# A four-layer graph network on one core: norms on ScalarE, GpSimd for more of the scalings, and a new order of the work

## The chip, the cores and the metric

The kernel runs on one core of a Trainium2 chip. The core has a matrix engine (TensorE, PE in the profile, with its weight loads as PEld), VectorE (DVE), ScalarE (ACT), GpSimd (POOL) and the DMA queues, here those of SyncE (SP) and ScalarE. They run side by side and wait for each other by semaphores. The metric is the device time of one execution in microseconds (us): 2461.91 is the median of three runs of the kernel before, which lie between 2461.11 and 2462.0.

## The reference

There are 16 graphs (batches) of 1024 nodes with 128 features each, and a dense 1024x1024 array adj for each graph. Four layers follow one another; each adds its result to x:

```
h = relu(layernorm(x));  x = x + L0(h, adj)   # three times: h=hW+b; ew = adj * cos(h_i, h_k); h = ew @ h (relu but for the last)
h = relu(layernorm(x));  x = x + L1(h, adj)   # adj^T h + (1+eps) h, then two dense products with relu, masked by node
h = relu(layernorm(x));  x = x + L2(h, adj)   # softmax over neighbours of tanh(s1_i + s2_k); a node without any keeps h
h = relu(layernorm(x));  x = L3(h, adj) + x   # e = (hA)h^T + its transpose, softmax, times adj, relu -> h'
                                              # i,f,o = sigmoid([h, h'] w);  o * tanh(sigmoid(i*h' + f*h))
```

All is in float32. The four norms, the lone nodes of layer 2 and the last line of layer 3 are what the change touches.

## The kernel before

**Tiling.** The 1024 nodes are NB = 8 blocks of P = 128, one node per partition. A tile 128x1024 holds one array of 1024 nodes by 128 features, block beside block. adj of a graph is loaded twice: transposed by 32x32 squares with DMA and VectorE (adjT, `turn`, used by layers 0, 2 and 3), and as it is (adjL, layer 1).

**Stages.** `layer0` to `layer3` write down the operations of one batch, in a loop over 16 batches. Each of the three products of layer 0, and layer 3, walks over eight tiles j: TensorE makes a row of the square (sq, L753), VectorE multiplies it with adjT (ew, L952, or e, L1169), TensorE sums up (acc, L815 or L826). As the square is symmetric, half of its blocks are taken from those above: copied by ScalarE (above, L785) and turned by TensorE (L763), or, in batches 1 to 13, one quarter by VectorE and DMA (L775, by_hbm, got).

**Order.** Nothing is issued as it is written. `op`, with its short forms `pe`, `act`, `dve` and `pool_op`, hands each operation to `Plan` with an assumed duration. `Plan.order` (L137) then plays the engines through: at each step it takes, among the operations ready on the engine that is free first, the one of lowest rank (due time of its batch, less the work behind it, less a lead from the table `LEADS`), assigns slots of the buffers (`POOLS`, and in `KINDS` limits for each kind, in all and for younger batches) and so fixes each engine's instruction stream. Batches up to `AHEAD` = 2 after the oldest are open at once. The due times are `PERIOD` apart, the last one only `LAST` after the one before. A `dve` operation with a true last argument, and every `pool_op`, take one shared "port" in this plan, so that two of them are never planned at once.

**Norms.** `layernorm` (L653) takes statistics on VectorE (L663, L672), the power -0.5 on GpSimd (`power`, L555), nb = -mean * rstd on VectorE (L682), and then scales: blocks 0 to 3 by VectorE (`scale_by_vector`, L689, one TENSOR_SCALAR a block, L691), blocks 4 to 7 by ScalarE (`scale_by_scalar`, L696, one ACTIVATE a block with relu, L698). `relu` (L712) clips the first half on ScalarE where hn itself is used again (L719). A branch on the letter "R" in `FLAGS` (L702) does all eight on ScalarE.

**Lone nodes.** In `layer2`, x += hn * alone for nodes without neighbours: eight SCALAR_TENSOR_TENSOR of VectorE (`add_scaled`, L637), or, with "P", two instructions of GpSimd (`on_pool`, L647).

**The end of a batch.** In `layer3`, `finish` (L1225) computes the gates (L1237, L1261, L1262), z = hn * f on GpSimd (L1265), z += h' * i (`scaled`, L1244), two tanh on ScalarE (L1241, L1242), and z * o + x (`scaled` again). `scaled` is eight SCALAR_TENSOR_TENSOR (L1255) or, with "P" or in the last two batches (`late`, "y"), a multiply and an add of GpSimd (L1248, L1249). For the last batch `finish` runs twice, for half of the nodes each ("h"). In the last two batches GpSimd also does the product e * adjT of the odd j of layer 3 ("z", L1190), which is VectorE's otherwise (L1194).

The letters that hold before are:

```
    FLAGS = set("Cabcdkxhyz")
    PERIOD, LAST, AHEAD, WINDOW = 60.0, 9.0, 2, 0.05
```

Of the kernel before, what the change touches and what calls it, by code (L numbers as in the profile page):

```python
# [8 lines left out]
F32 = mybir.dt.float32  # L9
# [5 lines left out]
P = 128  # L15
# [207 lines left out]
def tile_adj_preln(  # L223
# [66 lines left out]

    R = B * NB
# [22 lines left out]
    eye3 = const.tile([D, E3], F32, name="eye3")  # L314
    load_const(third, b3e[:, 0:D], L3_W_b.partition_broadcast(P))
    for g, (w, v) in enumerate(((L3_ig_w, L3_ig_b), (L3_fg_w, L3_fg_b), (L3_og_w, L3_og_b))):
        at = slice(D + g, D + g + 1)
        load_const(third, w3e[:, at], w[0, 0:D].rearrange("(p o) -> p o", o=1))
        load_const(third, eye3[:, at], w[0, D : 2 * D].rearrange("(p o) -> p o", o=1))
        load_const(third, b3e[:, at], v.partition_broadcast(P))  # L320
    for load_it in first:
        load_it()
# [10 lines left out]
    POOLS = {"adjT": 16, "adjL": 5, "x": 3, "big": 13, "above": 2, "got": 1, "bank": 8, "small": 29, "row": 8, "hbm": 3, "hrow": 2}  # L333
    KINDS = {
        "adjT": ("adjT", 16, 16), "adjL": ("adjL", 5, 5), "x": ("x", 3, 3), "w4": ("big", 10, 6),
        "chunk": ("big", 12, 4), "above": ("above", 2, 1), "got": ("got", 1, 1), "ps": ("bank", 8, 8),
        "acc": ("bank", 8, 8), "small": ("small", 7, 6), "row": ("row", 4, 2), "hbm": ("hbm", 3, 2),
        "hrow": ("hrow", 2, 1),
    }
    PERIOD, LAST, AHEAD, WINDOW = 60.0, 9.0, 2, 0.05  # L340

    LEADS = {
        "0 ACT hT": 10, "0 ACT hn": -27, "0 DVE hn": -7.5, "0 DVE mv": 18.5, "0 DVE nb": -2, "0 DVE st": -7,
        "0 PE ps": 6, "0 POOL rstd": -23, "00 ACT above": -218, "00 ACT hT": 68.5, "00 ACT hTn": -53.5,
        "00 ACT sq": -48, "00 DMA by": 63.5, "00 DMA got": -27.5, "00 DVE above": -233, "00 DVE ew": -9,
        "00 DVE h": -18.5, "00 DVE ss": -111, "00 PE acc0": -166.5, "00 PE ps": -134, "00 PE psP": -26,
        "01 ACT above": 3.5, "01 ACT hT": 55, "01 ACT hTn": -8.5, "01 ACT sq": 54.5, "01 DMA by": -23,
        "01 DMA got": 26, "01 DVE above": 4, "01 DVE ew": 108.5, "01 DVE h": -56, "01 DVE ss": 126.5,
        "01 PE acc0": -136, "01 PE ps": 9, "01 PE psP": -303.5, "02 ACT above": 5, "02 ACT hTn": -115.5,
        "02 ACT sq": 6.5, "02 DMA by": 38, "02 DMA got": -41, "02 DVE above": -10.5, "02 DVE ew": -116,  # L350
        "02 DVE h": -5, "02 DVE ss": -17, "02 DVE x": -78, "02 PE acc0": -116, "02 PE ps": -15, "02 PE psP": 12,
        "02 PE sq": 175, "02 POOL rn": 47.5, "1 ACT g": -36, "1 ACT hn": -48.5, "1 ACT y1": -1.5,
        "1 DMA adjL": -41.5, "1 DVE adjL": -57, "1 DVE hn": -11.5, "1 DVE mv": -94, "1 DVE nb": 152,
        "1 DVE st": -539.5, "1 DVE x": 119.5, "1 PE acc1": -1, "1 PE py": -157, "1 PE py2": -10.5,
        "1 POOL rstd": -12, "2 ACT e2": -4, "2 ACT h": 114.5, "2 ACT hfl": -3.5, "2 ACT hn": -82,
        "2 ACT hnT": -9, "2 DVE alone": 5, "2 DVE e2": 105, "2 DVE h": -2.5, "2 DVE hn": 2.5,
        "2 DVE hrow": -74.5, "2 DVE mv": 11.5, "2 DVE nb": 36.5, "2 DVE rden": 26.5, "2 DVE st": -3,
        "2 DVE x": -11, "2 PE acc2": 5.5, "2 PE p1": 1.5, "2 PE pf": 22, "2 PE ps": 23.5, "2 PE psP": -299.5,
        "2 POOL rstd": 4.5, "3 ACT above": 93, "3 ACT e3": 29, "3 ACT gT": 13.5, "3 ACT gate": -70,
        "3 ACT h3T": -6, "3 ACT hn": 9, "3 ACT hnT": 66.5, "3 ACT hp": -371, "3 ACT hs": -94, "3 ACT z": -137,  # L360
        "3 DMA by": -47.5, "3 DMA got": 34.5, "3 DMA z": -167.5, "3 DVE above": 23.5, "3 DVE e3": -253.5,
        "3 DVE gate": -473.5, "3 DVE h": -119, "3 DVE hn": -0.5, "3 DVE mv": -27.5, "3 DVE nb": 25,
        "3 DVE st": -150, "3 DVE top": -14, "3 DVE z": -942, "3 PE acc3": -134, "3 PE pg": -81, "3 PE ps": 54,
        "3 PE psN": -465.5, "3 PE psP": 3.5, "3 PE sq": 73, "3 POOL rstd": -109.5, "3 POOL z": -13.5,
        "T ACT adjT": -44, "T DMA adjT": 10.5, "T DVE adjT": -411.5, "0 ACT hT <0": -20.5, "0 ACT hT <1": 6,
        "0 ACT hT >0": 6, "0 ACT hT >1": 12, "0 ACT hn <0": -3, "0 ACT hn <1": 49, "0 ACT hn >0": 0,
        "0 ACT hn >1": 31, "0 DVE hn <0": -146.5, "0 DVE hn <1": -18, "0 DVE hn >0": -50, "0 DVE hn >1": 34,
        "0 DVE mv <0": -8.5, "0 DVE mv <1": 29.5, "0 DVE mv >0": 4, "0 DVE mv >1": -11, "0 DVE nb <0": 27,
        "0 DVE nb <1": -61, "0 DVE nb >0": -16.5, "0 DVE nb >1": 51.5, "0 DVE st <1": -11.5, "0 PE ps <0": 25.5,
        "0 PE ps <1": 4, "0 PE ps >0": 9, "0 PE ps >1": 22, "0 POOL rstd <0": 35, "0 POOL rstd <1": 12.5,  # L370
        "0 POOL rstd >0": -77, "0 POOL rstd >1": -19.5, "00 ACT above <0": -4, "00 ACT above <1": -60,
        "00 ACT above >0": -198.5, "00 ACT above >1": -41.5, "00 ACT hT <0": 1.5, "00 ACT hT <1": 11,
        "00 ACT hT >0": 21.5, "00 ACT hT >1": -18, "00 ACT hTn <0": -28.5, "00 ACT hTn <1": 60.5,
        "00 ACT hTn >0": -127, "00 ACT hTn >1": -97.5, "00 ACT params <0": -7.5, "00 ACT sq <0": 223,
        "00 ACT sq <1": 321.5, "00 ACT sq >0": -46, "00 ACT sq >1": 179.5, "00 DMA by <1": 0.5,
        "00 DMA got <1": -76, "00 DMA params <0": 12, "00 DVE above <1": -159, "00 DVE ew <0": 0,
        "00 DVE ew <1": -57.5, "00 DVE ew >0": -155, "00 DVE ew >1": -235.5, "00 DVE h <0": -3,
        "00 DVE h <1": -148.5, "00 DVE h >0": 45, "00 DVE h >1": -2.5, "00 DVE params <0": 60,
        "00 DVE ss <0": 109, "00 DVE ss <1": 12.5, "00 DVE ss >0": -8.5, "00 DVE ss >1": -228.5,
        "00 PE acc0 <0": -64, "00 PE acc0 <1": -216.5, "00 PE acc0 >0": -246, "00 PE acc0 >1": -266.5,  # L380
        "00 PE params <0": 101, "00 PE ps <0": 0, "00 PE ps <1": -36.5, "00 PE ps >0": 39, "00 PE ps >1": -91.5,
        "00 PE psP <0": 20, "00 PE psP <1": -2, "00 PE psP >0": 47, "00 PE psP >1": -187.5, "00 PE sq <1": 51,
        "00 PE sq >0": -4, "00 PE sq >1": 3, "01 ACT above <0": 49.5, "01 ACT above <1": -68.5,
# [127 lines left out]

    FLAGS = set("Cabcdkxhyz")

    LO, HI = 1, 2
    TINY = 0.09  # L520
    STT = 0.262

    def V(n, scalar=False):
# [605 lines left out]
    def layer3(b, xt, aT):  # L1129
# [77 lines left out]
        for s, (lo, hi) in enumerate(HALVES):  # L1207
            evict(acc[s], hpT, lo, hi, AF.Relu)
# [185 lines left out]
```

## Time and profile before

| | us |
|---|---|
| time, median of three | 2461.91 |
| span of the profiled run | 2462.7 |
| TensorE busy | 2397.5 |
| VectorE busy | 2106.1 |
| ScalarE busy | 1291.5 |
| GpSimd busy | 254.5 |
| scaling of norms, VectorE / ScalarE (256 instructions each) | 73.1 / 105.3 |
| lone nodes on VectorE (128) | 34.9 |
| last scalings on VectorE (112 + 112) | 30.5 + 30.6 |
| z = hn * f on GpSimd (15 whole, 2 halves) | 28.6 + 2.0 |

How to read it: busy time is what an engine spends on instructions, and a high share of it marks the engine to look at first. Here TensorE works for 97% of the span, so time taken from another engine counts only where TensorE (or, at the end, the output) waits for it. The granted clock of TensorE is 0.991 of full speed over the span. DMA is never short but in the first 100 us, when the parameters and the first graphs arrive.

### The profile page before, as it was taken

The page shows a single profiled execution, that of the slowest core. Times are in us where ns is not written, and L with a number is a line of the kernel's source. Part 1 is how long each engine was busy: PE and PEld are TensorE (multiplying, and loading weights), DVE is VectorE, ACT ScalarE, POOL GpSimd, SP SyncE. Part 2 cuts the span into 40 slices and gives each one's busy share as a digit, 9 for nine tenths or more (in the row PEclk, how much of TensorE's full clock was granted, in tenths as well). Part 3 has the DMA queues.
Part 4 walks back from the last instruction along what each step waited for, and adds up shares of the span by engine and source line. Part 5 has one row for each costly group of instructions (what it writes and reads, how often), then busy time and mean ns, then how long its engine had stood idle before and what let it go on. Part 6 is the DMA issues. An engine that isn't in the chain of part 4 may idle for free.

```text
span 2462.7 us, 34845 instructions
## 1 busy us (share of the span) xinstructions
PE 2397.5 (97%) x11946; PEld 1592.9 (65%) x11946; DVE 2106.1 (86%) x5232; ACT 1291.5 (52%) x2404; POOL 254.5 (10%) x155
## 2 busy tenths in 40 slices
PE   6999999999999999999999999999999999999985
PEld 3568576775756657576675766657576675765763
DVE  6758889888998989899898998989899898897585
ACT  4415564735546465464644646465464745656274
POOL 1001010100101101010010101101010010100025
PEclk9999999999999999999999999999999999999998
DMA  8731929658394764928649394774929646072000
GB/s 132 125 103 35 167 56 144 139 89 160 72 159 112 107 142 94 174 67 147 136 82 167 65 164 114 100 145 93 173 73 146 134 86 133 28 96 75 26 1 18
DMA packets 1129473, 263.35 MB, mean 107 GB/s; under 512 B 971856, under 2 KB 1112912, under 8 KB 1129296
## 3 DMA queue, kind: packets, MB, share of 16 engines
q1 hardware_dynamic: 1108368, 251.73, 57.3%
q10 hardware_dynamic: 20928, 9.40, 1.4%
q8 instruction: 94, 1.54, 0.3%
q14 instruction: 83, 0.68, 0.1%
HBM read 198.14 MB, written 62.91 MB: 106 GB/s over the span
## 4 chain that ended last, share of the span: by engine, by line
PE 86%; DVE 5%; DMA 4%; ACT 3%; SPq 1%; POOL 1%; issue 0%; POOLq 0%; DVEq 0%; ACTq 0%
PE acc L815 33%; PE sq L753 17%; PE acc L826 17%; PE psP L593 6%; PE sq L763 4%; PE py L1014 2%; PE py L603 2%; PE ps_hTn L562 2%; DMA adjT<-in_adj_dram 1%; DMA by_hbm<-above 1%; PE ps_hnT L562 1%; PE pg L603 1%; DVE ew L952 1%; PE psN L593 1%; SPq L872 1%; DMA got<-by_hbm 1%
## 5 line engine op out<-in xcount | busy, mean ns | idle before, releaser
L952 DVE SCALAR_TENSOR_TENSOR ew<-sq,rn,adjT 128x512 f32<-128x512 f32 x612 | 437.9, 741 | 92.8 <-ACT above L785 33.0
L815 PE MATMUL acc<-ew,h 128*128 128x512 f32 x1024 | 488.0, 598 | 8.6 <-DVE ew L952 8.3
L753 PE MATMUL sq<-hTn 128*128 128x512 f32 (+3 forms) x1152 | 432.3, 488 | 0.4 <-ACT hTn L615 0.3
L785 ACT COPY above<-sq 128x384 f32<-128x384 f32 (+3 forms) x432 | 167.6, 392 | 431.8 <-PE sq L763 257.4
L753 PEld LDWEIGHTS sq<-hTn 128*128 128x128 f32 x1152 | 198.8, 191 | 152.6 <-issue 104.3
L815 PEld LDWEIGHTS acc<-ew,h 128*128 128x128 f32 x1024 | 177.7, 191 | 164.8 <-issue 120.9
L555 POOL TENSOR_TENSOR rstd<-ve,mhalf 128x8 f32<-128x8 f32 x64 | 107.5, 1679 | 1572.5 <-DVE ve L674 1524.3
L826 PEld LDWEIGHTS acc<-h,ew 128*128 128x128 f32 x2048 | 243.1, 192 | 29.9 <-issue 17.3
L826 PEld LDWEIGHTS acc<-h,e 128*128 128x128 f32 x2048 | 240.5, 194 | 25.6 <-issue 13.3
L826 PE MATMUL acc<-h,ew 128*128 128x128 f32 x2048 | 252.3, 276 | 0.9 <-DVE ew L952 0.9
L826 PE MATMUL acc<-h,e 128*128 128x129 f32 x2048 | 243.1, 277 | 3.4 <-DVE e L1102 3.4
L815 PE MATMUL acc<-e,hs 128*128 128x512 f32 x512 | 242.1, 595 | 0.5 <-DVE e L1194 0.5
L883 ACT ACTIVATE adjT<-adjT 128x1024 f32<-128x1024 f32 x128 | 135.2, 1057 | 203.8 <-DVE adjT L880 136.2
L815 PE MATMUL acc<-adjL,hn 128*128 128x512 f32 x512 | 229.6, 593 | 0.1
L763 PEld LDWEIGHTS sq<-ident,above 128*128 128x128 f32 x960 | 125.2, 141 | 122.1 <-issue 79.2
L1185 ACT ACTIVATE e<-e,top 128x1024 f32<-128x1024 f32 x128 | 146.8, 1147 | 105.3 <-DVE top L1181 103.6
L763 PE MATMUL sq<-ident,above 128*128 128x128 f32 x960 | 175.5, 274 | 5.5 <-ACT above L785 5.4
L1102 DVE SCALAR_TENSOR_TENSOR e<-adjT,e 128x512 f32<-128x512 f32 x256 | 161.5, 685 | 14.6 <-ACT e L1098 14.4
L880 DVE STREAM_TRANSPOSE adjT<-adjT 128x1024 f32<-128x1024 f32 x128 | 154.5, 1223 | 14.5 <-DMA adjT<-in_adj_dram 13.9
L775 DVE STREAM_TRANSPOSE above<-sq 128x512 f32<-128x512 f32 x208 | 147.3, 709 | 21.6 <-PE sq L753 19.6
L815 PEld LDWEIGHTS acc<-adjL,hn 128*128 128x128 f32 x512 | 93.9, 190 | 102.8 <-issue 88.1
L1194 DVE TENSOR_TENSOR e<-e,adjT 128x512 f32<-128x512 f32 x240 | 157.2, 686 | 0.0
(129 smaller groups left out, 3534.2 us busy)
## 6 DMA issues: line engine op xcount, KB each, us to landing
adjT<-in_adj_dram SPq DMA_DIRECT2D x512, 128.0 KB, 4.2
adjL<-in_adj_dram SPq DMA_DIRECT2D x128, 512.0 KB, 5.0
by_hbm<-above SPq DMA_DIRECT2D x104, 512.0 KB, 4.1
got<-by_hbm SPq DMA_DIRECT2D x416, 128.0 KB, 3.9
x<-in_x_dram SPq DMA_DIRECT2D x15, 512.0 KB, 5.4
out_dram<-z ACTq DMA_DIRECT2D x15, 512.0 KB, 5.9
x<-in_x_dram SPq DMA_DIRECT2D x2, 256.0 KB, 4.4
out_dram<-z ACTq DMA_DIRECT2D x2, 256.0 KB, 2.3
```

The costliest lines, as they stand in the source:

```text
L593: nc.tensor.matmul(dst.t[:, (c - lo) * n : (c - lo + 1) * n], cols(srcT.t, c), w, start=True, stop=True)
L753: lambda: nc.tensor.matmul(dst.t[:, (first - lo) * P :], cols(leftT.t, j), span(rightT.t, first, hi), start=True, stop=True),
L763: nc.tensor.transpose(cols(dst.t, r), cols(above.t, p), ident)
L775: lambda: nc.vector.transpose(span(above.t, p, p + 4), read.t),
L785: lambda: nc.scalar.copy(span(above.t, p, p + hi - first), read.t[:, (first - lo) * P :]),
L815: lambda s=s, lo=lo, hi=hi: nc.tensor.matmul(acc[s].t, cols(h.t, at, w), span(ew.t, lo, hi), start=(j == 0), stop=(j == NB - 1)),
L826: nc.tensor.matmul(a.t[:, (c - lo) * n : (c - lo + 1) * n], cols(ew.t, c), h.t[:, j * w : j * w + n], start=(j == 0 and c == lo), stop=(j ...
L880: dve(V(N), [t], [t], lambda t=t: nc.vector.transpose(t.t, t.t), True)
L952: lambda view=view, ew=ew, rn=rn, j=j, lo=lo, hi=hi: nc.vector.scalar_tensor_tensor(by_block(span(ew.t, lo, hi), D, 4), view(), rn.t[:, j ...
L1102: lambda e=e, j=j, lo=lo, hi=hi: nc.vector.scalar_tensor_tensor(span(e.t, lo, hi), span(aT[j].t, lo, hi), 0.0, span(e.t, lo, hi), op0=ALU. ...
L1185: lambda e=e, top=top, tot=tot: nc.scalar.activation(e.t[:, 0:N], e.t[:, 0:N], AF.Exp, bias=top.t, accum_out=tot.t),
L1194: lambda e=e, j=j, lo=lo, hi=hi: nc.vector.tensor_mul(span(e.t, lo, hi), span(e.t, lo, hi), span(aT[j].t, lo, hi)),
```

## The change

The letters in `FLAGS` become "CabcdkxhPRzT". "y" goes, and three come:

- R: all eight blocks of each norm are scaled by ScalarE, with the relu in the same instruction, so that `relu` has nothing left to do.
- P: GpSimd adds the lone nodes in layer 2 and does both scalings at the end of layer 3.
- T: the last batch is an exception to that. VectorE ends it, the product hn * f included, which becomes one TENSOR_SCALAR a block; and the odd tiles of e * adjT in its layer 3 return to VectorE (batch 14 leaves them on GpSimd).

This is meant to relieve VectorE in the middle of the kernel, and to spare the end GpSimd's long instructions. GpSimd's adds are now planned with 2.37 us in place of 1.9, and its products e * adjT with 2.45 in place of 1.96. The order is made anew: other slot limits, other due times, and new values for all of `LEADS`. Other branches that come with the diff ("E" with `by_nodes` and `share`, "u" and "v" in `far`) are off; with these letters `far` is true for the same batches 1 to 13 as the condition it replaces.

```diff
-    POOLS = {"adjT": 16, "adjL": 5, "x": 3, "big": 13, "above": 2, "got": 1, "bank": 8, "small": 29, "row": 8, "hbm": 3, "hrow": 2}
+    POOLS = {"adjT": 16, "adjL": 5, "x": 3, "big": 13, "above": 2, "got": 1, "bank": 8, "small": 24, "row": 5, "hbm": 3, "hrow": 2}
     KINDS = {
-        "adjT": ("adjT", 16, 16), "adjL": ("adjL", 5, 5), "x": ("x", 3, 3), "w4": ("big", 10, 6),
-        "chunk": ("big", 12, 4), "above": ("above", 2, 1), "got": ("got", 1, 1), "ps": ("bank", 8, 8),
-        "acc": ("bank", 8, 8), "small": ("small", 7, 6), "row": ("row", 4, 2), "hbm": ("hbm", 3, 2),
+        "adjT": ("adjT", 16, 16), "adjL": ("adjL", 5, 5), "x": ("x", 3, 3), "w4": ("big", 11, 7),
+        "chunk": ("big", 10, 8), "above": ("above", 2, 1), "got": ("got", 1, 1), "ps": ("bank", 7, 5),
+        "acc": ("bank", 8, 5), "small": ("small", 7, 7), "row": ("row", 5, 5), "hbm": ("hbm", 3, 2),
...
-    PERIOD, LAST, AHEAD, WINDOW = 60.0, 9.0, 2, 0.05
+    PERIOD, LAST, AHEAD, WINDOW = 90.0, 11.0, 2, 0.02
     LEADS = {
...
-    FLAGS = set("Cabcdkxhyz")
+    FLAGS = set("CabcdkxhPRzT")
...
-        pool_op(1.9, [a, b], [dst], lambda: nc.gpsimd.tensor_add(by_block(dst.t), v(), by_block(b.t)))
+        pool_op(2.37, [a, b], [dst], lambda: nc.gpsimd.tensor_add(by_block(dst.t), v(), by_block(b.t)))
...
-            if ("5" in FLAGS or "z" in FLAGS and b >= B - 2) and j % 2:
-                pool_op(1.96, [e, aT[j]], [e], lambda e=e, j=j: nc.gpsimd.tensor_mul(e.t[:, 0:N], e.t[:, 0:N], aT[j].t))
+            if ("5" in FLAGS or "z" in FLAGS and (b == B - 2 if "T" in FLAGS else b >= B - 2)) and j % 2:
+                pool_op(2.45, [e, aT[j]], [e], lambda e=e, j=j: nc.gpsimd.tensor_mul(e.t[:, 0:N], e.t[:, 0:N], aT[j].t))
...
-        late = b >= B - 2
+        late = b == B - 2 if "T" in FLAGS else b >= B - 2
+        final = "T" in FLAGS and b == B - 1
...
-                if "P" in FLAGS or ("y" in FLAGS and late):
+                if not final and ("P" in FLAGS or ("y" in FLAGS and late)):
...
-                    pool_op(us, [blk(a, lo, hi, w), blk(c, lo, hi)], [blk(z, lo, hi)], lambda: nc.gpsimd.tensor_add(part(z), part(a, w), part(c)))
+                    pool_op(us + 0.4 * n / NB, [blk(a, lo, hi, w), blk(c, lo, hi)], [blk(z, lo, hi)], lambda: nc.gpsimd.tensor_add(part(z), part(a, w), part(c)))
...
+            if final:
+
+                def of_x():
+                    for k in range(lo, hi):
+                        nc.vector.tensor_scalar_mul(cols(z.t, k), cols(hn.t, k), gate.t[:, 3 * k + 1 : 3 * k + 2])
+
+                dve(n * 0.17, [blk(hn, lo, hi), at], [blk(z, lo, hi)], of_x)
+            else:
+                pool_op(
+                    0.2 + 1.7 * n / NB, [blk(hn, lo, hi), at], [blk(z, lo, hi)],
+                    lambda: nc.gpsimd.tensor_mul(part(z), part(hn), per_node(of(1), n)),
+                )
```

## The prediction

> **What bounds the kernel now.** I read the page's busy table first, then the same table cut into stretches, then the chain of waits at the end, then the timeline around GpSimd's instructions.
>
> From the page, the row of engine totals:
>
> ```profile
> PE 2397.5 (97%) x11946; PEld 1592.9 (65%) x11946; DVE 2106.1 (86%) x5232; ACT 1291.5 (52%) x2404; POOL 254.5 (10%) x155
> ```
>
> Busy time of each engine by stretch (stretch, length, then PE, weight loads, DVE, ACT, POOL, with instruction counts; last the granted clock, DMA share, GB/s):
>
> ```profile
> 0.00:100.00 100.00, 78.51 (x322) 46.29 (x323) 73.12 (x171) 46.68 (x92) 12.16 (x13) 0.97 1.02 156
> ...
> 300.00:2100.00 1800.00, 1794.45 (x8933) 1189.43 (x8932) 1616.37 (x4021) 964.03 (x1800) 163.94 (x97) 1.00 0.66 120
> ...
> 2350.00:2400.00 50.00, 40.86 (x246) 32.72 (x245) 42.56 (x101) 37.03 (x62) 9.68 (x5) 0.90 0.00 1
> ...
> 2437.00:2463.00 26.00, 0.03 (x1) 0.00 (x0) 3.46 (x4) 5.67 (x10) 20.94 (x15) 0.55 0.14 40
> ```
>
> TensorE is full through the middle. It is short of work in three places: the first 100 us (21.5 idle), 2350 to 2400 (9.1 idle) and the last 26 us, when GpSimd works alone. The ends of matmuls are modelled, so I also added the start-to-start distances of all matmuls. In the chain 24 of the 512-wide ones take 10.30 us, 0.429 each, and 128 of the 128-wide take 14.29 us, 0.112 each. At its usual spacing (0.429, 0.322, 0.216 and 0.109 to 0.112 us by width) all TensorE work sums to 2359 us. The other 104 us are: 11.9 before the first matmul; 18 more lost in the first 100 us; 5 in 200 to 300; about 18 between 300 and 2100, or 1 us in each 148 us batch; 2 in 2100 to 2330; 15.6 around 2355 to 2395; 26 after the last matmul; and some 7 of jitter of a few ns.
>
> The end of the chain of waits (start, us, what), where GpSimd's 15 us begin:
>
> ```profile
> 2434.80 1.80 PE psN L593 x16
> ...
> 2436.62 0.50 ACT hp L1216
> ...
> 2437.14 1.72 DVE gate L1237
> ...
> 2439.12 1.61 DVE gate L1262
> ...
> 2440.78 2.16 POOL z L1249
> ...
> 2454.13 1.86 POOL z L1248
> ...
> 2456.04 2.37 POOLq L1390
> ```
>
> Fifteen GpSimd instructions run one behind another here: five for batch 14 (128x1024), ten for the two halves of batch 15. The two gate instructions on 128x12 take 1.7 and 1.6 us; that is no work but a wait for GpSimd.
>
> **What the Trainium skill says.** "GPSIMD Engine Reference", Specifications, says that GpSimd's SBUF interfaces are shared with VectorE, with contention for VectorE instructions in a 2-port mode or with two SBUF inputs. The trace agrees in part. Timeline (start, us, instruction):
>
> ```profile
> 2386.25 3.15 DVE L691 TENSOR_SCALAR hn<-x,mv,rstd 128x128 f32<-128x128 f32 x4
> ...
> 2386.41 2.38 POOL L1190 TENSOR_TENSOR e<-e,adjT 128x1024 f32<-128x1024 f32 x1 [0.70 <-PE sq L763]
> ```
>
> Four TENSOR_SCALAR take 3.15 us instead of some 1.1: one sits 2.38 us behind the GpSimd product. A TENSOR_TENSOR on adjL (L997, median 0.286) took 1.303 in the same position. But the 44 SCALAR_TENSOR_TENSOR of 128x128 that overlap GpSimd average 0.345 us, against a median of 0.344 for the others, although they too have two SBUF inputs. So I charge stalls to TENSOR_SCALAR and TENSOR_TENSOR only.
>
> The same page, Engine selection, puts elementwise work with two inputs at about twice VectorE's time. Here: multiply 1.91 and add 2.16 to 2.34 us, 4.2 us a pair, for what eight VectorE instructions at 0.26 spacing do in 2.1. It agrees.
>
> "ScalarE: Activation LUTs", What ACT_TABLE_LOAD costs, gives 186 ns + 0.833 ns per element and 93 ns per pointer operand; 128 elements with scale and bias pointers make 479. L698 has a median of 480 and 0.385 spacing. It agrees.
>
> **The change, part by part, per batch.**
>
> *Norms on ScalarE (R).* Removed: 16 TENSOR_SCALAR (L691, 256 in all, 73.1 us busy, so 4.6 of VectorE) and three relus (L719, 0.62 each). Added on ScalarE: 16 activations at 0.385, 6.2. Net for ScalarE +4.3 on 80.7, or 57% of 148. A norm is done about 1.5 us later (eight in a row, 3.2, where each engine did four in 1.1 and 1.65 side by side). In the middle the other batches in flight hide that, since TensorE hardly waits. In the first batch, hn is ready 1.5 us later; TensorE then waits for adj tiles from DMA until 66 us anyway (DMA share 1.02 in the first 100 us), so 0. In the last batch's layer 3 the old version needed 3.15 us because of the stall, the new one 3.2: 0.
>
> *Lone nodes on GpSimd (P, layer 2).* Removed: eight SCALAR_TENSOR_TENSOR (34.9 us in all, 2.2 a batch). Added: 1.9 + 2.3 on GpSimd, beside the eight tiles of attention that must be done before x is added to again: 0 on the path.
>
> *Last scalings on GpSimd (P, layer 3).* Removed in batches 0 to 13: 16 SCALAR_TENSOR_TENSOR (30.6 + 30.5 over 14 batches, 4.4 each). Added: two multiplies and two adds, 8.5. Behind the last add only the output DMA waits, and the slot of x. Batch 14 keeps GpSimd as before.
>
> Sum in the middle: VectorE sheds 11.1 of 131.6 us and has 15.1 idle (1800 - 1616 = 184 over 12.2 batches). GpSimd rises by 12.7 to some 26 of 148. Six more GpSimd instructions of about 2.1 us can each hold one TENSOR_TENSOR: at most 12.7 us of stall, at least 0. So VectorE is at worst where it is now, and at best 11 us freer. TensorE, not VectorE, sets the 148 us, so only the 1 us per batch of leftover waits can be won. I take 0.2 per batch, 3 in all; the ends are 0 and 13.
>
> *Last batch ended by VectorE (T).* Two parts. First, its four odd tiles of layer 3 return to VectorE: 8 x 0.686 = 5.5 us more, in a stretch (2370 to 2430) where VectorE is 90 to 100% busy in most 10 us windows. Against this stand 2.2 (lone nodes), 1.1 (half a norm) and 2 of stall, and TensorE is full from 2395 to 2436. I take 0 on the path, ends -2 and +5.
>
> Second, the tail. From the last matmul at 2436.6: hp 0.5, gate 0.18, tanh 0.22, gate 0.17 with 0.2 of hops, 1.25 in all. Then for each half four TENSOR_SCALAR at 0.255 (1.1) and four SCALAR_TENSOR_TENSOR at 0.26 (1.15): 4.5 for both. Then the second half's two tanh, 0.63 + 0.72 + 0.1 = 1.45, with the first half's last scaling beneath; then four more, 1.15. That ends at 2436.6 + 8.35 = 2445.0, where the page has GpSimd's last end at 2458.4: **13.4 us less**. If batch 14's five GpSimd instructions still begin at 2436.9, they and the two tanh between take 1.9 + 1.9 + 2.2 + 2.2 + 1.9 + 2.3 = 12.4 and end at 2449.3: **9.1 less**. I take 11, ends 6 (if TENSOR_SCALAR of batch 15 queue behind those instructions) and 14.
>
> *Order made anew.* Slot limits, the spacing of due times (60 to 90) and all leads change, so the instruction streams differ throughout. The old trace does not price that. Best: all 18 us in the middle and 5 at 2355 to 2395 are won. Worst: I allow 1.5 us more per batch, as much again as is lost today and half more. Value taken: 0.
>
> Sum: 2461.9 - 11 - 3 = **2448**.
>
> **The rivals.**
>
> *Gaps close too.* The freed VectorE and the new order remove 13 of the 18 us in the middle and 5 around 2380: 2461.9 - 11 - 18 = 2433. For it: VectorE's ew (L952) ends 1.6 of the 5.3 us that the view of waits names for TensorE there. Against: the most frequent one is TensorE's mirrored blocks behind ScalarE's copy (L763 behind L785, 3.7 us), and ScalarE gets busier.
>
> *The tail is given back.* The extra 5.5 us of VectorE work falls in its full stretch, or batch 14 ends last behind a longer GpSimd queue: 2461.9 - 6 + 5 = 2461.
>
> *The new order costs more than the tail.* 1.5 us in each of 14 batches, through GpSimd's holds on VectorE and ScalarE's later norms, is 21 against 11: 2472. For it: the 2.38 and 1.30 us stalls are real, and GpSimd's load doubles. Against: three batches are interleaved, and TensorE starves nowhere between 300 and 2100.
>
> **How the numbers follow.** Forecast 0.49, gaps close 0.21, tail given back 0.10, slower 0.20. Faster by over 0.2% (below 2457) is the first two, 0.70; within it (2457 to 2467) the third with a little of its neighbours, 0.10; above, 0.20. The range runs from 2430, below which lies a third of the second case, to 2468, which leaves out over half of the slower one.
>
> **What would show it.** The two busy rows of SCALAR_TENSOR_TENSOR on z and the one on x<-hn gone except for batch 15; VectorE near 1950 us busy, ScalarE near 1365, GpSimd near 420; TensorE still about 2395 with 16 to 19 us between its last matmul and the end, and the chain's last pieces on VectorE. Wrong steps would show as TensorE idle above 1 us per batch between 300 and 2100, as TENSOR_TENSOR means well over 0.69, or as a last GpSimd instruction within 5 us of the end. Above all it is the new order that could make the prediction wrong.

## The result, and the profile after

The changed kernel takes **2502.74 us**, the median of four runs (2497.59 to 2505.4). Its ratio to the kernel before, run beside it, is **1.0165, with a 95% interval of 1.0147 to 1.0183**: slower by about 41 us, where the prediction had 14 us faster.

The page's row of engine totals, kernel after (busy us, share, instructions):

```profile
PE 2416.0 (97%) x11946; PEld 1597.0 (64%) x11946; DVE 2036.1 (81%) x4656; ACT 1349.8 (54%) x2612; POOL 429.3 (17%) x229
```

The work went where it was meant to go. VectorE has 576 instructions and 70 us less, ScalarE and GpSimd have more, nearly as forecast. TensorE still shows 97%, of a longer span. Busy time by stretch, kernel after (columns as in the prediction):

```profile
0.00:100.00 100.00, 76.92 (x319) 45.41 (x320) 69.03 (x158) 49.00 (x102) 12.13 (x13) 0.98 0.92 157
300.00:2100.00 1800.00, 1765.13 (x8710) 1167.86 (x8709) 1533.82 (x3464) 974.02 (x1889) 323.58 (x168) 0.99 0.62 117
2350.00:2400.00 50.00, 49.61 (x299) 37.01 (x298) 28.06 (x115) 21.46 (x41) 5.29 (x3) 1.00 0.10 32
2437.00:2502.00 65.00, 45.23 (x171) 23.69 (x169) 44.71 (x115) 33.21 (x68) 12.94 (x7) 0.94 0.05 17
```

The second row is the one to read. In the same 1800 us of the middle, TensorE got through 8710 matmuls where it had done 8933: 2.5% of 1800 us, some 45 us of its work, is missing. Yet VectorE is *less* busy there, 1533.8 against 1616.4. None of the other engines is full; something makes TensorE wait although they have time.

I summed the start-to-start distances of the matmuls again. The usual spacing gives some 2359 us in every kernel here; what is over it is time lost between matmuls (us, profiled runs):

| | span | before first matmul | lost between matmuls | of this 300 to 2100 | after start of last matmul |
|---|---|---|---|---|---|
| before | 2462.7 | 11.9 | 66.4 | 18.4 | 25.9 |
| after | 2501.6 | 11.3 | 120.7 | 66.3 | 10.9 |
| after, nb on GpSimd | 2445.1 | 11.6 | 64.1 | 11.9 | 10.9 |

The tail won 15.0 us. The middle lost 47.9, and some 6 went elsewhere. (The third row belongs to an experiment below.) The end of the chain of waits, kernel after (start, us, what), shows the won tail: the last pieces are VectorE's, and no GpSimd instruction is among them.

```profile
2489.18 1.45 PE psN L598 x12
...
2490.65 0.83 ACT hp L1241 x2
...
2491.51 0.17 DVE gate L1268
...
2491.83 0.87 DVE z L1298 x4
...
2497.73 0.53 DVE z L1286 x2
```

For the middle, the view of TensorE's waits, kernel after (who waits for whom: us in all, times, longest):

```profile
PE pf L1062 <- DVE hrow L1055: 18.0, 13, 1.8
PE ps_hnT L567 <- ACT hn L703: 16.0, 11, 1.5
PE ps_hT L567 <- ACT hn L703: 11.3, 1, 11.3
```

The third is the first batch's start and is there in every kernel. The first two are new (the kernel before has no wait on `hrow`, and 0.7 us on `hn` there), come at most once a batch, and both belong to layer 2. Here is one batch of the second kind, from the timeline of the kernel after (start, us, engine, line, instruction; in brackets the idle time before it and who ended it):

```profile
1065.45 3.62 DVE L957 SCALAR_TENSOR_TENSOR ew<-got,rn,adjT 128x512 f32<-128x512 f32 x2
...
1066.16 2.35 POOL L1304 TENSOR_TENSOR z<-hn,gate 128x1024 f32<-128x1024 f32 x1
...
1068.60 2.50 POOL L1280 TENSOR_TENSOR z<-hp,z 128x1024 f32<-128x1024 f32 x1
...
1068.99 2.13 DVE L687 SCALAR_TENSOR_TENSOR nb<-mv,rstd 128x8 f32<-128x8 f32 x1
...
1071.15 3.19 ACT L703 ACTIVATE hn<-x,nb,rstd 128x128 f32<-128x128 f32 x8 [2.92 <-DVE nb L687]
1071.70 1.49 PE L567 MATMUL ps_hnT<-ident,hn 128*128 128x128 f32 x4 [1.45 <-ACT hn L703]
```

GpSimd runs the end of the batch ahead: hp * gate (from 1064.30), hn * gate, and the add, back to back. Beside them VectorE has two `ew` that should take 0.75 each and take 3.62 (1.30 and, overlapping a little, 2.39): the first is held until hp * gate ends, the second until hn * gate ends. Next is `nb`, the tiny -mean * rstd of layer 2's norm, 128x8. It begins at 1068.99, when GpSimd's add is at work, and ends with it at 1071.1. All eight ACTIVATE of the norm need `nb`, so ScalarE stands 2.92 us. TensorE, whose order the program fixes, stands 1.45 for the first block, and then takes four turns in 1.49 us, at ScalarE's pace of 0.385 apiece, though it could do one in 0.11. What `nb` costs, and what it should cost, is in one row of the view of that tile (min/median/max ns):

```profile
L687 DVE SCALAR_TENSOR_TENSOR nb<-mv,rstd x64: 124/160/2135, 10.5 to 2445.6; 128x8 f32<-128x8 f32 x64
```

The other wait, ten microseconds later in the same timeline:

```profile
1078.59 2.35 POOL L656 TENSOR_TENSOR x<-hn,x 128x1024 f32<-128x1024 f32 x1
1078.60 2.42 DVE L1055 TENSOR_SCALAR hrow<-hsum 128x128 f32<-128x128 f32 x1
...
1081.16 0.46 PE L1062 MATMUL pf<-w2f,hrow 128*128 128x128 f32 x2 [1.83 <-DVE hrow L1055]
```

`hrow` (normally 0.28 us) starts some 0.02 us after GpSimd's add of the lone nodes and lasts as long as that does. So it is in nine batches; in two it started 0.08 us *before* the add, and was not held (0.29).

I count as a hold what an instruction takes beyond the usual time of its kind, if that is over 0.1 us. In all, `ew<-got` was held 26.4 us (23 times), `hrow` 22.7 (14), `nb` 21.8 (11) and the sums of squares `ss` 4.2 (11), and a few others 7.7 together: 82.8 us in this kernel against 6.5 before. The profile counts held time as busy time. So holds don't show as idleness; they show in the mean of a shape. Two groups, same operation and size, first of the kernel before, then of the kernel after (instructions, then busy us and mean ns):

```profile
L952 DVE SCALAR_TENSOR_TENSOR ew<-sq,rn,adjT 128x512 f32<-128x512 f32 x612 | 437.9, 741 | 92.8 <-ACT above L785 33.0
L952 DVE SCALAR_TENSOR_TENSOR ew<-got,rn,adjT 128x512 f32<-128x512 f32 x156 | 112.1, 746 | 10.4 <-DMA got<-by_hbm 6.0 <-DMA adjL<-in_adj_dram 3.3 <-issue 0.5
...
L957 DVE SCALAR_TENSOR_TENSOR ew<-sq,rn,adjT 128x512 f32<-128x512 f32 x612 | 430.7, 736 | 94.8 <-ACT above L790 59.0
...
L957 DVE SCALAR_TENSOR_TENSOR ew<-got,rn,adjT 128x512 f32<-128x512 f32 x156 | 136.9, 912 | 31.1 <-DMA got<-by_hbm 28.2
```

The first operation reads sq from PSUM, the second reads got from SBUF, and only the second grew. Here are the groups that matter of the VectorE instructions that began while a GpSimd instruction of 128x1024 was at work in the kernel after (over 0.03 us behind its start, over 0.1 us ahead of its end):

| | times | ns, median |
|---|---|---|
| h<-psP (one input in PSUM) | 69 | 343, as ever |
| ew<-sq (one input in PSUM) | 43 | 742, as ever |
| ss<-sq (TENSOR_REDUCE, one input) | 25 | 673, as ever |
| ew<-got (two inputs, SBUF) | 22 | 1300 (11) and 2390 (11) in place of 750 |
| nb (two inputs, SBUF) | 11 | 2130 in place of 160 |
| ss (TENSOR_SCALAR, SBUF) | 11 | 587 in place of 160 |
| hrow (TENSOR_SCALAR, SBUF) | 5 | 1250 in place of 280 |
| adjL (TENSOR_TENSOR, SBUF) | 2 | 2000 in place of 280 |

(Nine others of `hrow`, as the one above, began within 0.03 us of the add's own start, and took 2400 to 2420.) The Trainium skill has this rule: "SBUF — State Buffer", Who interferes with whom, says that VectorE's second port pair is shared with GpSimd as an exclusive lock, that a VectorE instruction with two SBUF inputs contends there with a GpSimd instruction that reads SBUF, and so does one in a 2-port mode, which `tensor_scalar` can enter. It says that an instruction outside these modes with at most one SBUF input doesn't contend. These rows agree with it (`nb` 2130 ns, `h<-psP` 343 as ever); whether the TENSOR_SCALARs ran in such a mode no run here shows. One thing differs, and there the measurement decides: beside GpSimd's powers, 128x8 and 1.64 us long, which read SBUF as well, nothing was held. The 21 `ew<-got` that began beside one in the kernel before have a median of 746 ns, and the 35 `e<-adjT,e` (two inputs in SBUF) in the kernel after 679, as ever.

### The profile page after: what moved, and what is told of

Same layout as the page of the kernel before. It is cut to its first block, busy times and chain, and to the rows that moved or that the text cites. A ratio compares the mean times of both kernels' runs of the same rounds, so it can differ in the third digit from the quotient of the medians.

```text
span 2501.6 us, 34454 instructions
## 1 busy us (share of the span) xinstructions
PE 2416.0 (97%) x11946; PEld 1597.0 (64%) x11946; DVE 2036.1 (81%) x4656; ACT 1349.8 (54%) x2612; POOL 429.3 (17%) x229
## 4 chain that ended last, share of the span: by engine, by line
PE 83%; DVE 8%; ACT 4%; DMA 2%; SPq 1%; issue 1%; ACTq 0%; DVEq 0%
PE acc L820 30%; PE acc L831 18%; PE sq L758 17%; PE psP L598 4%; DVE ew L957 3%; PE sq L768 3%; PE py L1019 2%; PE py L608 2%; PE ps_hTn L567 1%; ACT hn L703 1%; DVE hrow L1055 1%; PE pg L608 1%; DVE nb L687 1%; PE psN L598 1%; PE ps_hnT L567 1%; PE p L1088 1%
## 5 line engine op out<-in xcount | busy, mean ns | idle before, releaser
L957 DVE SCALAR_TENSOR_TENSOR ew<-sq,rn,adjT 128x512 f32<-128x512 f32 x612 | 430.7, 736 | 94.8 <-ACT above L790 59.0
L820 PE MATMUL acc<-ew,h 128*128 128x512 f32 x1024 | 477.7, 599 | 5.9 <-DVE ew L957 5.8
L820 PEld LDWEIGHTS acc<-ew,h 128*128 128x128 f32 x1024 | 183.1, 193 | 179.9 <-issue 130.6
L703 ACT ACTIVATE hn<-x,nb,rstd 128x128 f32<-128x128 f32 x512 | 205.7, 482 | 134.9 <-DVE nb L687 88.7
L820 PE MATMUL acc<-adjL,hn 128*128 128x512 f32 x512 | 237.0, 593 | 1.1 <-ACT hn L703 1.1
L957 DVE SCALAR_TENSOR_TENSOR ew<-got,rn,adjT 128x512 f32<-128x512 f32 x156 | 136.9, 912 | 31.1 <-DMA got<-by_hbm 28.2
```

Source lines behind the costliest of these rows:

```text
L703: nc.scalar.activation(cols(hn.t, c), cols(xt.t, c), AF.Relu, bias=nb.t[:, c : c + 1], scale=rstd.t[:, c : c + 1])
L820: lambda s=s, lo=lo, hi=hi: nc.tensor.matmul(acc[s].t, cols(h.t, at, w), span(ew.t, lo, hi), start=(j == 0), stop=(j == NB - 1)),
L957: lambda view=view, ew=ew, rn=rn, j=j, lo=lo, hi=hi: nc.vector.scalar_tensor_tensor(by_block(span(ew.t, lo, hi), D, 4), view(), rn.t[:, j ...
```

## The experiments

The order of the work is fixed by the planner from assumed durations and buffers. In every kernel below these stay as they were, and only what an operation issues differs; so the work that stays on an engine keeps its order there, except where it says that `nb` moves. The edits are shown shortened. Two theories stood at the start. **Holds**: two small VectorE instructions, held by GpSimd, stop TensorE. **Rival**: the new order, or ScalarE's double load of norms, is late by itself, and the holds lie beside the path.

**1. `hrow` on ScalarE, in the kernel after.**

```diff
-  nc.vector.tensor_scalar_add(hrow.t, hsum.t[:, 0:1].to_broadcast([P, D]), hsum.t[:, 1:2])
+  nc.scalar.activation(hrow.t, hsum.t[:, 0:1].to_broadcast([P, D]), AF.Identity, bias=hsum.t[:, 1:2])
```

> The changed kernel in its own order, with one instruction of each batch on another engine: hrow (128x128, one a batch) is computed by ScalarE in place of VectorE. Theory 'held instructions': TensorE's pf waits 18.0 us in 13 batches because hrow stands behind GpSimd's additions; those waits go, the time falls by 15 to 22 us, to 2481 to 2488. Theory 'order' (the loss lies in the new order as such and in ScalarE's later norms): TensorE finds another wait in the same place, and the time stays at 2498 to 2505.

Measured: 2479.53 us, ratio 1.0069 (1.0053 to 1.0086), 23.2 us less than the kernel after for sixteen instructions, a little more than the theory of holds had said. The view of TensorE's waits has 0.6 us left at `pf`, and still has the other in full:

```profile
PE ps_hnT L567 <- ACT hn L703: 16.0, 11, 1.5
PE ps_hT L567 <- ACT hn L703: 11.3, 1, 11.3
```

**2. `nb` on GpSimd, in the kernel after.** There it stands in GpSimd's own queue, right after the power that makes rstd and ahead of the long instructions; ScalarE turns its sign.

```diff
-  nc.vector.scalar_tensor_tensor(nb.t, mean, -1.0, rstd.t, op0=ALU.mult, op1=ALU.mult)
+  nc.gpsimd.tensor_tensor(nb.t, mean, rstd.t, op=ALU.mult)
+  nc.scalar.activation(nb.t, nb.t, AF.Copy, scale=-1.0)
```

> The changed kernel in its own order, with nb (128x8, one a norm) computed by GpSimd right in its own queue and negated by ScalarE, in place of VectorE. Theory 'held instructions': nb no longer stands behind the end of the batch before (2.13 us itself, and another 2 to 3 behind an ew that is held too); hn of layer 2 comes some 4 us earlier, TensorE's waits for it (16.0 us in 11 batches, and about 1 us more in each for the pace of ScalarE) go: 15 to 25 us less, 2477 to 2487. Theory 'order': ScalarE's eight activations in a row are what TensorE waits for; under 5 us less.

Measured: **2447.91 us, ratio 0.994 (0.9925 to 0.9955)**: 54.8 us less than the kernel after, more than twice what was expected. The timeline of this kernel at the same place:

```profile
1045.96 0.65 POOL L687 TENSOR_TENSOR nb<-mv,rstd 128x8 f32<-128x8 f32 x1
1046.58 2.41 POOL L1307 TENSOR_TENSOR z<-hn,gate 128x1024 f32<-128x1024 f32 x1
1046.65 0.21 ACT L688 ACTIVATE nb<-nb 128x8 f32<-128x8 f32 x1 [2.59 <-POOL nb L687]
...
1047.94 3.19 ACT L706 ACTIVATE hn<-x,nb,rstd 128x128 f32<-128x128 f32 x8
...
1049.85 0.60 PE L567 MATMUL ps_hnT<-ident,hn 128*128 128x128 f32 x4
```

GpSimd takes `nb` *ahead* of its long product, the norm starts 1.3 us after, and by the time TensorE comes to the turns all four blocks are there: 0.60 us and no wait. Its view of waits shows that the other wait went too, although `hrow` was not touched:

```profile
PE pf L1065 <- DVE hrow L1058: 1.4, 3, 0.6
```

The timeline of the same batch shows by how little:

```profile
1055.54 0.29 DVE L1058 TENSOR_SCALAR hrow<-hsum 128x128 f32<-128x128 f32 x1
1055.62 2.43 POOL L656 TENSOR_TENSOR x<-hn,x 128x1024 f32<-128x1024 f32 x1
```

In eleven batches `hrow` now begins 0.07 to 0.08 us ahead of the add, where in nine it had begun 0.02 to 0.03 us after it. It does so in experiments 4 and 5, too, where `nb` is free as well; so the second wait hung on the first, and that is the term that the expectation missed. But the margin is a tenth of a microsecond, and what shifts it isn't shown: that part of the gain, some 20 us, owes something to luck.

The holds themselves haven't gone. They still come to 48.1 us in this kernel, 30.6 of them on 24 instructions of adjL, for which TensorE doesn't wait.

**3. Both edits.**

> The two edits together: hrow on ScalarE, nb on GpSimd, order kept. Theory 'held instructions': the gains add up to 30 to 45 us, so 2457 to 2472, and TensorE's idle time between 300 and 2100 us falls from 35 to under 10. Theory 'order': over 2490.

Measured: 2446.62 us, ratio 0.9935 (0.992 to 0.9949), the fastest kernel of the study and below the 2457 to 2472 that the theory of holds had said, but within the interval of experiment 2. Taken alone the two edits gave 23.2 and 54.8; together they give 56.1, since the second already removes what the first removes. The middle stretch of this kernel:

```profile
300.00:2100.00 1800.00, 1798.78 (x8946) 1191.36 (x8945) 1545.70 (x3483) 1020.72 (x2023) 348.42 (x224) 1.00 0.65 120
```

TensorE is at 1798.8 of 1800 with 8946 matmuls, 13 more than the kernel before. The rival theory is out as the cause of the loss: the order, and the norms on ScalarE, are the same as in the kernel after.

**4. Only the place of `nb`.** In the kernel after, layer 2's `nb` is issued up to six VectorE instructions earlier, as soon as its inputs are there.

```diff
   ordered = plan.order()
+  for n in [o for o in ordered if o.key == "2 DVE nb"]:
+      ...  # i: the first VectorE operation behind n's inputs whose move breaks no dependency and no slot
+      ordered.insert(i, ordered.pop(j))
```

> The changed kernel with one thing moved: nb of layer 2 stays on VectorE, but is issued up to six instructions earlier, at the place where rstd is ready by the plan, before GpSimd begins the end of the batch before; all else keeps its order and its engine. Theory 'place' (what costs is that nb is issued where GpSimd's three instructions hold VectorE): as good as nb on GpSimd, 2443 to 2453. Theory 'engine' (VectorE simply carries too much there, and nb on GpSimd relieved it): over 2480.

Measured: 2465.53 us, ratio 1.0014 (1.0007 to 1.0021), 37 us less than the kernel after, and between what the two theories had said. Timeline of this kernel:

```profile
1050.46 0.16 DVE L687 SCALAR_TENSOR_TENSOR nb<-mv,rstd 128x8 f32<-128x8 f32 x1
...
1055.75 2.50 POOL L1280 TENSOR_TENSOR z<-hp,z 128x1024 f32<-128x1024 f32 x1
...
1056.14 2.26 DVE L1002 TENSOR_TENSOR adjL<-adjL,ident_e 128x128 f32<-128x128 f32 x1
...
1058.33 1.40 DVE L957 SCALAR_TENSOR_TENSOR ew<-sq,rn,adjT 128x512 f32<-128x512 f32 x2
...
1059.12 1.98 PE L820 MATMUL acc<-ew,h 128*128 128x512 f32 x4 [1.29 <-DVE ew L957]
```

`nb` is free again at 0.16. But the add now holds the next instruction with two SBUF inputs, a 128x128 one of adjL that is in no hurry, for 2.26 us, and behind that in VectorE's queue stands the `ew` that TensorE needs. Its waits show it: 17.5 us in 14 batches.

```profile
PE acc L820 <- DVE ew L957: 17.5, 14, 2.4
```

So the place of `nb` matters, and a hold moved is not a hold removed.

**5. The last scalings back on VectorE, in the kernel after.** In batches 0 to 13, eight SCALAR_TENSOR_TENSOR for each of the two, at the place of GpSimd's adds.

```diff
-  nc.gpsimd.tensor_mul(part(a, w), part(a, w), per_node(of(g), n))
-  nc.gpsimd.tensor_add(part(z), part(a, w), part(c))
+  for k in range(lo, hi):  # b < 14
+      nc.vector.scalar_tensor_tensor(cols(z.t, k), cols(a.t, k, w), s(k), cols(c.t, k), op0=ALU.mult, op1=ALU.add)
```

> The changed kernel in its own order, with the two last scalings of layer 3 of batches 0 to 13 back on VectorE (16 SCALAR_TENSOR_TENSOR each, at the place where the plan had GpSimd's additions). Theory 'place': two of GpSimd's three long instructions before nb are gone, so nb is free again; VectorE carries 4.4 us more in a batch of which it has over 20 us to spare: 2445 to 2465. Rival: the relief of VectorE was worth something and its 61 us of work come back onto the path: over 2480.

Measured: 2463.64 us, ratio 1.0005 (0.9996 to 1.0014), 39 us less than the kernel after, as the theory of the place had said: two of the three GpSimd instructions that held VectorE are gone, among them the add that held `nb`, and with them the waits on `hn` but the first batch's. The holds come to 13.7 us in all. It is no win over before either, since now VectorE's block of eight (2.15 us) stands ahead of an `ew` that TensorE needs:

```profile
PE acc L820 <- DVE ew L957: 15.7, 13, 2.8
```

**6. The kernel before with one part each.** Norms: all eight blocks of each norm on ScalarE, `relu` issues nothing, and `nb` is issued ahead of the norm where it stood behind the first half. Last scalings and lone nodes: two GpSimd instructions at the place of eight of VectorE's (the last scalings in batches 0 to 13). Last batch: VectorE does the odd e * adjT, hn * f and both scalings of batch 15.

```diff
-  scale_by_vector(*HALVES[0])                          # norms
+  scale_by_scalar(*HALVES[0])
-  add_scaled(xt, D, 0, NB, hn, 0, D, alone, 0, xt, True)   # lone nodes
+  nc.gpsimd.tensor_mul(by_block(hn.t), by_block(hn.t), per_node(alone.t))
+  nc.gpsimd.tensor_add(by_block(xt.t), by_block(hn.t), by_block(xt.t))
-  nc.gpsimd.tensor_mul(part(z), part(hn), per_node(of(1), n))   # last batch (b == 15), likewise its scalings
+  for k in range(lo, hi):
+      nc.vector.tensor_scalar_mul(cols(z.t, k), cols(hn.t, k), gate.t[:, 3 * k + 1 : 3 * k + 2])
```

Norms alone:

> The kernel before in its own order, with only the norms' first halves on ScalarE as well (nb issued just before them where it came later). The forecast put it at 0 on the path, being hidden by the other batches. If ScalarE's eight activations at 0.385 us set the pace of TensorE's transposes (0.11 each), some 1 us a norm shows: for three norms in 16 batches up to 50 us, 2465 to 2510; else within 5 us of before.

Last scalings alone:

> The kernel before in its own order, with only the last scalings of layer 3 in batches 0 to 13 on GpSimd. Theory 'place': GpSimd's four instructions more hold whatever two-input instruction of VectorE stands there; in an order that wasn't made for them the time rises by 5 to 40 us. Rival, the forecast's own view: TensorE is the bound and VectorE has the slack; within 5 us of before.

Lone nodes alone:

> The kernel before in its own order, with only the lone nodes of layer 2 on GpSimd. Theory 'place': in the old order hrow stands right after the eight instructions that go, so it now meets GpSimd's addition as in the changed kernel; pf waits up to 2 us in most batches: 2466 to 2495. Rival, the forecast: 0 on the path, within 5 us of before.

Last batch alone:

> The kernel before in its own order, with only the last batch's part of the change: VectorE does its odd products of layer 3 and ends it. The forecast's step for the tail says 6 to 14 us less, 2447 to 2455. If VectorE's full stretch between 2370 and 2430 pays for it, the time stays within 5 us of 2461.5.

Measured:

| before, with | us | ratio (95%) |
|---|---|---|
| norms on ScalarE | 2499.44 | 1.0159 (1.0142 to 1.0176) |
| last scalings on GpSimd | 2470.95 | 1.0042 (1.0027 to 1.0057) |
| lone nodes on GpSimd | 2465.32 | 1.0010 (1.0003 to 1.0016) |
| last batch ended by VectorE | 2459.26 | 0.9983 (0.9976 to 0.999) |

The norms cost 38 us in the old order, with hardly a hold (3.8 us in all). One batch in the timeline of that kernel:

```profile
1118.14 1.65 ACT L698 ACTIVATE hn<-x,nb,rstd 128x128 f32<-128x128 f32 x4 [0.89 <-DVE nb L682]
...
1118.89 1.27 PE L562 MATMUL ps_hnT<-ident,hn 128*128 128x128 f32 x4
...
1120.84 1.16 PE L593 MATMUL psP<-w,hT 128*128 128x128 f32 x8 [0.67 <-ACT hT L615]
```

TensorE's four turns take 1.27 us, at ScalarE's pace again, and then it waits for `hT`, an eviction that stands behind the norm in ScalarE's queue. Over its usual spacing TensorE loses in the middle 13.9 us at `ps_hnT`, 13.1 at `psP` and 8.7 at the mirrored blocks, 35.7 in all, where the kernel before loses some 9 at the last two and next to nothing at the first. That explains some 26 us; the rest is spread out. The time lies in the wide range that was expected (2465 to 2510), and the forecast's 0 does not hold in this order.

GpSimd's lone nodes do hold VectorE here: adjL for 21.6 us in ten batches, and `hrow` for 14.5 in thirteen:

```profile
L1055 DVE TENSOR_SCALAR hrow<-hsum x16: 275/1444/1448, 202.8 to 2351.0; 128x128 f32<-128x128 f32 x16
```

But the time rises by under 3 us. No wait of TensorE's `pf` on `hrow` shows in this kernel, and on adjL its weight loads wait 1.3 us in all. So the theory of the place was right about the hold and wrong about its price, and the forecast's 0 is right within 5 us. The last scalings cost 9 us, at the low end of what that theory had said (5 to 40).

The last batch's part is worth only 4 us here, less than the 6 to 14 that were expected (time after the start of the last matmul: 20.9 us against 25.9). Its chain of waits shows why:

```profile
2436.10 0.50 ACT hp L1223
...
2436.62 1.65 DVE gate L1244
...
2438.54 1.69 DVE gate L1278 x2
2440.25 3.56 DVE z L1253 x8
...
2450.24 1.57 DVE z L1260 x6
```

In the old order batch 14's GpSimd instructions still run here, and hold VectorE's gates (1.65 in place of 0.17) and its TENSOR_SCALARs (3.56 for eight, in place of 0.22 each). The new order has batch 14 out of the way by then, and the same edit ends 10 us sooner.

**7. One part taken out of the changed kernel with `nb` on GpSimd.** Norms: the first halves of layers 0, 2 and 3 return to VectorE, clipped later by ScalarE. Last scalings as in 5. Lone nodes: VectorE's eight at the place of GpSimd's add.

```diff
+  (scale_by_vector if lo == 0 and not k.endswith("_1") else scale_by_scalar)(lo, hi)   # norms
-  nc.gpsimd.tensor_mul(v(), v(), per_node(of_node()))                                  # lone nodes
-  nc.gpsimd.tensor_add(by_block(dst.t), v(), by_block(b.t))
+  for c in range(NB):
+      nc.vector.scalar_tensor_tensor(cols(dst.t, c), cols(a.t, c, w), of_node()[:, c : c + 1], cols(b.t, c), op0=ALU.mult, op1=ALU.add)
```

Norms taken out:

> Against a_nb (2447.9): the changed kernel with nb on GpSimd, order kept, and the first halves of the norms of layers 0, 2 and 3 back on VectorE (layer 1 stays; ScalarE clips the half later, before it is used again). Theory 'the order absorbs it': ScalarE's norms cost 38 us in the old order, but the new one issues them early enough; 2440 to 2455. Rival: they cost here what they cost there, and the time falls below 2430.

Last scalings taken out:

> Against a_nb (2447.9): nb on GpSimd, order kept, and the last scalings of batches 0 to 13 back on VectorE. Theory 'place': without the held nb, GpSimd's scalings are free and VectorE's are in the way of one ew that TensorE waits for (1.2 us a batch as in the run without it): 2450 to 2465. Rival: every instruction of GpSimd costs by its holds; below 2443.

Lone nodes taken out:

> Against a_nb (2447.9): nb on GpSimd, order kept, and the lone nodes of layer 2 back on VectorE (eight instructions, 2.1 us, where the plan had GpSimd's addition). Theory 'place': hrow is no longer held, but the 2.1 us stand in VectorE's queue at the start of layer 2, ahead of what TensorE needs next: 2445 to 2465. Rival: GpSimd's holds on hrow and ss still cost; below 2443.

Measured, where the whole is 2447.91:

| without | us | ratio to before (95%) | part is worth |
|---|---|---|---|
| norms on ScalarE | 2483.48 | 1.0085 (1.0071 to 1.0098) | 36 us |
| last scalings on GpSimd | 2463.81 | 1.0008 (1.0 to 1.0016) | 16 us |
| lone nodes on GpSimd | 2482.93 | 1.0086 (1.0072 to 1.01) | 35 us |

All three signs are the reverse of experiment 6. Only the last scalings came out as expected; for the norms and the lone nodes neither theory had it. The first wait of TensorE in the kernel without GpSimd's lone nodes, and one batch of it in the timeline:

```profile
PE pf L1071 <- DVE hrow L1064: 33.4, 11, 3.0
...
1067.06 1.91 POOL L1288 TENSOR_TENSOR z<-z,gate 128x1024 f32<-128x1024 f32 x1 [3.82 <-ACT z L1282]
...
1067.46 3.49 DVE L658 SCALAR_TENSOR_TENSOR x<-hn,alone,x 128x128 f32<-128x128 f32 x8
```

VectorE's eight instructions now stand ahead of `hrow` in its queue, and TensorE waits up to 3 us in eleven batches. Of the 3.49 us of the eight, 1.3 are a hold: the first one takes 1.66 us in place of 0.34, behind GpSimd's z * gate. So some 14 of the 33.4 us are again GpSimd's doing.

Without the norms on ScalarE, `hrow` is held once more (14 times, 16.0 us in all), and one wait of TensorE says so:

```profile
PE pf L1069 <- DVE hrow L1062: 11.3, 13, 1.4
```

The edit itself has a share in that: GpSimd's hn * alone has to wait for the clip that ScalarE does just ahead of it, and runs when `hrow` comes up. The 36 us are thus not the price of scaling on VectorE alone. Each order was made for one mix of work, and a part put into or taken out of a fixed order mostly costs something. These tables thus say what a part is worth in that order, and no more; no order was made anew for each mix.

## Why the prediction was wrong

**Stalls: the step that failed.** "So I charge stalls to TENSOR_SCALAR and TENSOR_TENSOR only." This rested on 44 SCALAR_TENSOR_TENSOR of 128x128 that overlap GpSimd in the trace before and take no longer, "although they too have two SBUF inputs". They have not. Of the 44, 40 are h<-psP and 4 are x<-py, and psP and py lie in PSUM. I took the operation's name for its operands, and for their sake set aside what I had just quoted on two SBUF inputs. Read rightly, these 44 say nothing of `nb` and `ew<-got`: in the kernel before no SCALAR_TENSOR_TENSOR with two inputs in SBUF began beside a GpSimd instruction of 128x1024 or 128x512 at all. To exempt them had no evidence, and in the kernel after they were held for 48 of the 82.8 us.

The kernel itself had the distinction. `nb`, adjL, and `ew` where it reads got are marked for the plan's "port", which keeps them clear of GpSimd in planned time; `ew<-sq`, `hrow` and `ss` are not marked. So `hrow` and `ss` were never kept clear, and for the marked ones nothing on the chip enforces the plan: the trace shows `nb` and GpSimd's add side by side.

**"VectorE is at worst where it is now": the step that followed.** The bound was on throughput, one hold of 2.1 us for each of six added GpSimd instructions, 12.7 us a batch. It held: the holds came to 82.8 us, some 5 a batch, and VectorE's busy time over the run fell by 70 us all the same. But what a hold costs is not VectorE's time. It is how late the held instruction's result is, with the work that stands behind it in a fixed order. `nb` works 0.16 us and was held in 11 batches, for 21.8 us in all, behind two `ew` that were held as well; taking it out of that place gained 55 us (experiment 2), of which 23 are those of `hrow` (experiment 1), which came free with it. The two waits named above are 34.0 us, and the three turns at ScalarE's pace, 3 x (0.385 - 0.11) = 0.8 in 11 batches, 9 more: 43 us, nearly all of it in the middle, where 48 were lost. "TensorE, not VectorE, sets the 148 us" was true of the kernel before, and ceased to be.

**Norms on ScalarE: 0 on the path.** Wrong for the old order (38 us, experiment 6), right for the new one: with `nb` free no wait of TensorE on `hn` is left but the first batch's and one of 1.1 us, and the part is worth having there. What failed was the reasoning: "In the middle the other batches in flight hide that" holds, as I read these runs, only if TensorE's queue has their work placed ahead of the norm's turns. The prediction never asked what stands at the head of that queue.

**Lone nodes and last scalings on GpSimd: 0.** In the changed order, with `nb` freed, taking them out costs 35 and 16 us. With `nb` on VectorE the last scalings hold it: without them it isn't held (experiment 5). The lone nodes' add holds `hrow`. The prediction's "It agrees" on GpSimd's speed also compares unlike things: two GpSimd instructions with a fused one of VectorE. One by one it is 1.91 to 2.34 us against 2 x 0.686 for a VectorE TENSOR_TENSOR of the same size.

**The tail: 11 forecast, 15.0 found.** The mechanism was right, its end on VectorE too. The mis-sized term was batch 14's: I let its five GpSimd instructions begin at the last matmul; the new order had them done before. Where they are not done, the same edit gives 5 (experiment 6). So the upper end, 14, was too low by one microsecond, and the value taken allowed for a collision that the order avoids; the sum without it, 13.4, was nearer.

**Order made anew: 0, worst 1.5 us a batch.** The worst case, 2472, was the right rival (slower, through GpSimd's holds on VectorE), but I sized it by what was lost already, and the loss was 48 us in 12 batches, about 4 each. The order itself is no worse than the old one: with `nb` on GpSimd and the order left as it is, the middle loses less than before (11.9 us against 18.4).

**Busy times.** Forecast VectorE 1950, ScalarE 1365, GpSimd 420; found 2036.1, 1349.8 and 429.3. VectorE's excess of 86 us is, to within 10 us, the holds that came on top (82.8 against 6.5 before). "TENSOR_TENSOR means well over 0.69" was named as a sign; the sign came on SCALAR_TENSOR_TENSOR instead (912 against 736).

The forecast of 2448 is what the change gives with `nb` freed, 2447.91. That the two agree so closely is luck: in the profiled runs the tail gives 15.0 in place of 11 and the middle 6.5 in place of 3, and some 4 us are lost elsewhere. The one cost that it set at nothing was larger than all the others.

The parts alone, in the old order, sum to 1.0159 + 1.0042 + 1.0010 + 0.9983 - 3 = 1.0194, near the 1.0165 of the whole. That is a coincidence: the norms lose there by ScalarE's pace and queue, and the whole loses by holds on `nb` and `hrow`.

What stays open: whether an order planned for each mix would show a part worth more or less than the tables say, and why `hrow` wins its race with the add once `nb` is free.

## What to carry to other kernels

Before moving work to GpSimd, list the VectorE instructions that come up beside it and look where each *operand* lies, not only what the operation is called: those with two inputs in SBUF, or a plain TENSOR_SCALAR from SBUF to SBUF, can be held for the whole of a long GpSimd instruction, as here for those of 128x1024. Then ask of each what waits behind it; a hold of 2 us on work with slack was free here (adjL), and on a 0.16 us instruction at the head of a chain TensorE paid for it in 11 of 16 batches. Such small instructions did better on ScalarE (`hrow`), or in GpSimd's own queue ahead of its long work (`nb`).

## What the runs showed of the hardware that was not expected

- **One instruction slips through between two holds.** GpSimd's instructions follow one another within 0.1 us, and VectorE gets one instruction with two SBUF inputs done, then the next is held until the next GpSimd instruction ends. So in the batches shown a row of GpSimd instructions slows VectorE to one such instruction for each of GpSimd's: one `ew<-got` behind hp * gate, the next behind hn * gate, then `nb` behind the add. The time goes into the *duration* of the VectorE instruction; its idle time in the profile stays small.
- **GpSimd is slowed too.** Its product hn * gate takes 1.91 us in four batches, and 2.35 in the eleven where an `ew<-got` that was held has just gone ahead of it (in the case above that worked for 0.54 us after hp * gate had ended at 1066.21); the add behind it runs from 2.17 to 2.51.
- **Tens of nanoseconds decide.** `hrow` begun 0.08 us ahead of the add ran free (0.29, two batches), and begun 0.02 to 0.03 us after it took 2.40 to 2.42 (nine).
- **Not every GpSimd instruction holds.** Its powers on 128x8 last 1.64 us, and 35 `e<-adjT,e` that began beside one in the kernel after kept 679 ns.
